# A two-layer transformer on one core: another fixed order for the second layer's steps

## The chip, the cores and the metric

The kernel runs on one core of a Trainium2 chip. A core has five engines with a queue of instructions each: TensorE (PE in the profile; its weight loads are shown apart as PEld), VectorE (DVE), ScalarE (ACT), GpSimd (POOL) and SyncE (SP, which here only starts DMAs). Each engine works off its own queue in order and waits at an instruction until what that instruction needs is there; while it waits, all that stands behind it in the queue waits too. The metric is the device time of one execution in microseconds (us): lower is better.

## The reference

The input x has 8 sequences of 256 rows of 512 values; a context of the same shape goes with it. Two layers follow each other, each with an attention and a feed-forward block that are added to x:

```python
x = x + tanh(g_xattn[0]) * causal_attention(layernorm(x), ctx, ctx)          # 16 heads of 32
x = x + tanh(g_ffn[0])   * ternary_ffn(layernorm(x), gate_up, proj)          # hidden 2048
x = x + tanh(g_xattn[1]) * cross_attention(layernorm(x), ctx, q_w, k_w, ...)  # 16 heads of 32
h = layernorm(x); h = h + out_8bit(silu(gate) * value)                       # hidden 2048
x = x + tanh(g_ffn[1]) * h
```

The change concerns the last three lines, "layer 1". There the queries are a linear layer of the normed x with an RMS norm behind it; each head's scores go through a softmax over 256 keys of the context; the result is projected and added. The feed-forward block quantizes its input and its hidden activation to 8 bits, each row by the row's own largest value: `scale = 127 / max|u|`, `round(u * scale)`. So a row's hidden values can only be quantized when all 2048 of them are there.

## The kernel before

Rows lie in 16 tiles `xs[0..15]` of 128 rows; a batch b (a sequence) is the two tiles 2b and 2b+1. Layer 1 is a software pipeline over batches. Pass b (of `for b in range(B)` at L1278) does the feed-forward block of batch b's two tiles (`first` = `feed1[2b]`, `second` = `feed1[2b+1]`) and, between its matmuls, parts of the attention of later batches.

*The order by hand.* `at(b, (n, step), ...)` puts a step at time b + n/16, and `timeline(*jobs)` (L1304) calls all steps sorted by these times. A pass has 16 units, and each unit begins with a gate product (`glu`, below); a step at 8.6 in `at(b, ...)` is emitted behind gate 8 of pass b, and one at 24.2 behind gate 8 of pass b+1. Steps from `at(b - 1, ...)` with n = 7.3 thus belong to the attention of batch b, emitted a pass ahead of its gates. PE executes its matmuls in exactly this order of emission. The queues of the other engines are put in order when the program is built, by the Tile framework's scheduler, which may move their instructions against each other as far as dependencies allow; on the chip each queue then is fixed.

*The steps of layer 1*, with the lines that the profile names:
- `glu(k)`, the gates: 8 matmuls (zT by gv weights) into one of two PSUM banks "gu"; ACT copies the bank to `gv` (L1186). After each odd one ACT takes a tanh (L1190), and DVE makes the gated value u from it (L1191, L1193) and its row maximum (L1194). 16 gates make a pass: 8 pairs, four for each of the two tiles. `gv` and `t1` have two buffers each, `u` two.
- `Feed1.done`: `quantize` takes the maximum over u (L1203 to L1206 on DVE: the scale), rescales u on ACT (L1232, two halves) and rounds it on POOL (L1233) into `uq`, of which there is one; two steps `turn` transpose uq by DMA into `uT` (L1238); two steps `project` multiply 8 chunks each into a bank ("o" for the first tile of a batch, "py" for the second), and behind the second half `store` adds the bank to x on DVE (L1223) and writes x out. `second.last` replaces these at the very end, with transposes on PE and four quarters.
- `Feed1.ready`: the norm ahead of the block (L1137 and L1143 on POOL, L1145 to L1151 on DVE, then L1153 and L1154 on POOL), and a DMA transpose of its result into `zT`.
- `Attention1.ready`: layer norm, turn on PE, load of keys and values, the query linear (`first(0)`, `first(1)`: matmuls "lin", L696 on DVE, the square on ACT L697), its norm (`scale`, L706), and the turn of the queries.
- `looks`: `scores(g)` for the four groups of heads (queries by keys, row maximum L415 on DVE), `parts` (the maxima in pieces, POOL L427 to L434, tile `mz`) and `shift` (turned on PE as "nt").
- `weighs`: four times `exps(g)` (scores turned round, exponential on ACT L481) and `weigh(g)` (32 matmuls into the one bank "o", copied by ACT L505; from g = 1 on POOL adds the sums, L508), in the order exps0, exps1, weigh0, exps2, weigh1, exps3, weigh2, weigh3.
- `Attention1.done`: `invert` (reciprocal on DVE, L1008), `divide` (spreads the inverses on PE into "inv" banks that take the places of "o" and "py", multiplied on DVE L1022), and two steps `add` (output projection, L1029).

PSUM has eight banks: two pairs "s" (scores, turns, exponentials), two "gu", one "o", one "py". A product into "o" or "py" has to wait until the last reader of that bank is done, be it `store`'s L1223, a copy L505, or L1022 and L1029.

Of the kernel before, what the change touches and what calls it, by code (L numbers as in the profile page):

```python
# [45 lines left out]
ALU = mybir.AluOpType  # L46
# [4 lines left out]
P = 128  # L51
B, S, D = 8, 256, 512
NT = B * S // P
NH, HD = 16, 32
DC = D // P
# [34 lines left out]
def flamingo_kernel(  # L90
# [24 lines left out]
    nc = tc.nc  # L115
# [10 lines left out]
    def bank(tag, shape=(P, 512), dtype=F32, name=None):  # L126
        pool, n = part_ps[tag]
        return pool.tile(list(shape), dtype, tag=tag, name=name or tag, bufs=n)
# [15 lines left out]
    def reach(i, n):  # L144
        assert stage.get(i, 0) == n - 1, (i, n)
        stage[i] = n
# [114 lines left out]
    pe = Tensor()  # L261
# [84 lines left out]
    def linear(dst, srcT, i, w):  # L346

        for c in range(DC):
            pe.matmul(
                dst,  # L350
                lhsT=srcT[:, c, i * P : (i + 1) * P],
                rhs=w(c),
                start=(c == 0),
                stop=(c == DC - 1),
            )


    class Attention:
# [3 lines left out]
        n = 0  # L362
# [150 lines left out]
                [*(lambda g=g: self.scores(g) for g in range(DC)), self.parts, self.shift],  # L513
            )

        def weighs(self):


            def exps(g):
                self.exps(g)  # L520
                ps[g] = self.p

            ps = {}
            steps = [lambda: exps(0)]
            for g in range(DC):
                if g + 1 < DC:
                    steps.append(lambda g=g: exps(g + 1))
                steps.append(lambda g=g: self.weigh(g, ps.pop(g)))
            return self.counted(self.nready + DC + 2, steps)

        def finish(self, steps):
# [2 lines left out]
    class Attention0(Attention):  # L534
# [21 lines left out]
        def done(self):  # L556
            def add():

                t = pair((P, 2, D), name="back")
                sums = bank("o", (P, 2, P), name="sums")  # L560
                for i in range(2):
                    rows = slice(i * P, (i + 1) * P)
                    for c in range(DC):
                        pe.transpose(
                            t[:, i, c * P : (c + 1) * P], self.oT[:, c, rows], ident
                        )
                    pe.transpose(sums[:, i, :], self.sums[:, rows], ident)
                inv = small.tile([P, 2, DC, 4], F32, tag="inv", name="inv", bufs=2)
                nc.vector.reciprocal(
                    inv, sums.rearrange("p i (r g e) -> p i g r e", r=4, g=DC)[:, :, :, :, 0]  # L570
                )
                for i in range(2):
                    xt = xs[2 * self.b + i]
                    w = self.oT[:, 2 * i : 2 * i + 2, :].rearrange("p c t -> p (c t)")
                    nc.vector.tensor_tensor(
                        w.rearrange("p (h c) -> p h c", h=NH),
                        t[:, i, :].rearrange("p (h c) -> p h c", h=NH),
                        inv[:, i].rearrange("p g r -> p (g r)").unsqueeze(2).broadcast_to([P, NH, HD]),
                        ALU.mult,
                    )  # L580
                    nc.vector.scalar_tensor_tensor(
                        xt, w, tg[:, 0:1], xt, ALU.mult, ALU.add
                    )
                    reach(2 * self.b + i, 1)

            return self.finish([add])
# [19 lines left out]
    def at(b, *steps):  # L606

        return [(b + n / 16, b + n / 16, [step]) for n, step in steps]
# [151 lines left out]
    with ExitStack() as part:  # L760
# [16 lines left out]
        a, z = att0[0], att0[1]  # L777
# [151 lines left out]
    def measure1(u):  # L929
        seen[0] += 1  # L930
        w = load1(u)
        a = q1.tile([P, QW], BF, tag="q", name="a1", bufs=2)
        behind(nc.scalar.activation(a, w, AF.Abs, accum_out=l1sum[:, u : u + 1]), block["A"])
# [17 lines left out]
    def quantize1(u):  # L951

        seen[1] += 1
        assert seen[0] == n1
        w = load1(u)
        _, dst, k = units1[u]
        ins = nc.gpsimd.tensor_scalar(w, w, wscale[:, k : k + 1], MAGIC, ALU.mult, ALU.add)  # L957
        behind(ins, block["P"])
        hold1()
        q = q1.tile([P, QW], BF, tag="q", name="q1", bufs=2)  # L960
        nc.gpsimd.tensor_scalar(q, w, 1.0, -MAGIC, ALU.mult, ALU.add)  # L961

        def hold():
            q8 = q1.tile([P, QW], F8, tag="q8", name="q8", bufs=2)
            nc.vector.tensor_scalar(q8, q, 1.0, -1.0, ALU.min, ALU.max, saturate=False)
            nc.sync.dma_start(out=dst, in_=q8.bitcast(U8))

        left.append(hold)
# [6 lines left out]
    class Attention1(Attention):  # L975
# [30 lines left out]
        def done(self):  # L1006
            def invert():
                nc.vector.reciprocal(self.oT[:, DC + 1, :], self.sums)  # L1008

            def divide():  # L1010
                for k in range(2):
                    w = bank(("o", "py")[k], (P, 2, S), name="inv")
                    for j in range(2):
                        pe.matmul(
                            w[:, j, :],
                            lhsT=spread[:, 2 * k + j, :],
                            rhs=self.oT[:, DC + 1, :],
                            start=True,
                            stop=True,
                        )  # L1020
                    cols = self.oT[:, 2 * k : 2 * k + 2, :]
                    nc.vector.tensor_tensor(cols, cols, w, ALU.mult)  # L1022

            def add(i):
                xt = xs[2 * self.b + i]
                nc.gpsimd.tensor_tensor(xt, xt, rob, ALU.add)
                t = bank(("o", "py")[i], name="proj")
                linear(t, self.oT, i, lambda c: wo[:, c, :])
                nc.vector.scalar_tensor_tensor(xt, t, tg[:, 1:2], xt, ALU.mult, ALU.add)  # L1029
                reach(2 * self.b + i, 3)  # L1030

            return self.finish([invert, divide, lambda: add(0), lambda: add(1)])

    att1 = [Attention1(b) for b in range(B)]
    x2 = ctx.enter_context(tc.tile_pool(name="x2", bufs=1, side="right", reuse_waits="tile"))
# [6 lines left out]
    with ExitStack() as part:  # L1042
# [4 lines left out]
        def rows(b):  # L1047
# [3 lines left out]
        jobs = [  # L1051
            (0.5, 3.0, [lambda u=u: measure1(u) for u in range(n1)]),
            (3.05, 3.05, [scales1]),
            (3.1, 6.5, [lambda u=u: quantize1(u) for u in range(n1)]),
            (6.6, 6.6, [hold1]),
        ]
# [44 lines left out]
    spread = w1p.tile([P, DC, P], F32, name="spread")  # L1101
# [176 lines left out]
    jobs = []  # L1278
    for b in range(B):
        first, second, a = feed1[2 * b], feed1[2 * b + 1], att1[b]  # L1280
        end = b == B - 1
        jobs += at(b, *((k, step) for k, step in enumerate(first.glus() + second.glus())))

        far = {B - 1: (15.9, 15.9), B - 2: (15.95, 15.95), B - 3: (13.2, 17.3)}.get(b, (13.2, 18.2))
        jobs += at(b, *zip((7.4 if b == B - 2 else 8.6, 9.6, 9.8, *far), first.done()))
        if end:
            jobs += at(b, (16.0, second.last))
        else:
            far = {B - 2: (23.9, 23.9), B - 3: (21.2, 22.2)}.get(b, (21.2, 24.2))
            jobs += at(b, *zip((17.4, 18.4, 18.6, *far), second.done()))  # L1290
        if b >= 2:

            late = 15.6 if b == 2 else 16.2
            jobs += at(b - 3, *zip((3.6, 12.2, 12.5, 14.2, late, 16.5, 18.9), a.ready()))
            jobs += at(b - 2, *zip((4.4, 6.4, 7.4, 9.3, 10.4, 14.1), a.looks()))
        if b >= 1:
            steps = (-0.8, 0.6, 2.3, 2.5, 3.2, 3.4, 4.2, 5.0) if end else (-0.8, 1.2, 3.2, 3.4, 4.2, 5.6, 6.2, 7.2)
            jobs += at(b - 1, *zip(steps, a.weighs()))
        steps = (5.1, 6.9, 7.6, 8.2) if end else (7.3, 9.2, 10.2, 11.2)
        jobs += at(b - 1, *zip(steps, a.done()))  # L1300
        for n, f in zip((7.7, 8.4) if end else (10.3, 13.0), (first, second)):
            norm, turn = f.ready()
            jobs += at(b - 1, (n, norm), (n + 1.7, turn))
    timeline(*jobs)  # L1304
# [52 lines left out]
```

## Time and profile before

| | us |
|---|---|
| median of 3 runs | 1248.93 (1246.83 to 1250.46) |
| the profiled execution, its device time | 1244.33 |
| its span in the profile | 1242.6 |
| layer 1 begins at about | 780 |
| second weighing done, passes in turn | 811.79, 869.8, 930.1, 990.24, 1050.7, 1110.98 |
| inverses of the last attention on PE | 1173.65 |
| first gate of the last pass | 1196.68 |

The six times of the second weighing mark the pipeline's passes: after the first they follow each other by 60.1 to 60.5 us. In the profile's timeline each line has a start, a duration, the engine, the line of the kernel, the operation and its operands; in brackets stands how long the engine had been idle before and which instruction released it. The view by windows gives for a stretch of time the busy time of each engine and the clock that TensorE was granted, as a share of full speed.

### The profile page before, as it was taken

How to read it: one execution, taken by the hardware profiler on the slowest of the kernel's cores; microseconds unless marked ns; L12 is line 12 of the kernel's file. 1: busy time of each engine (PE TensorE's matmuls, PEld its weight loads, DVE VectorE, ACT ScalarE, POOL GpSimd, SP SyncE). 2: the span in 40 equal slices, each digit the busy share in tenths (PEclk: the TensorE clock that was granted, in tenths of full speed). 3: DMA queues.
4: the chain of work that ended last, by engine and by line, in shares of the span. 5: the costliest groups of instructions: out<-in, count | busy, mean ns of one | idle time of the engine just before them, and what ended most of it. 6: DMA issues, size and time to landing. Idle time of an engine off the chain costs nothing.

```text
span 1242.6 us, 29878 instructions
## 1 busy us (share of the span) xinstructions
PE 1113.8 (90%) x12466; PEld 725.7 (58%) x12565; DVE 823.0 (66%) x1776; ACT 611.2 (49%) x1108; POOL 550.0 (44%) x821
## 2 busy tenths in 40 slices
PE   7988977799999897888999998899999999999976
PEld 3444433577777666666666775455555555555553
DVE  5677797764656455375654645777777777768684
ACT  3446547356575533433344453356464645464663
POOL 3333224353343556465564424826263535424250
PEclk9998888899999998999999999999999999999998
DMA  8343424622333233223222002311212121211231
GB/s 320 127 137 114 158 85 119 221 61 96 120 99 118 64 99 82 82 70 95 84 76 66 19 18 71 109 52 31 64 35 60 35 61 35 61 35 31 39 51 43
DMA packets 101767, 103.91 MB, mean 84 GB/s; under 512 B 61312, under 2 KB 72576, under 8 KB 101632
## 3 DMA queue, kind: packets, MB, share of 16 engines
q1 hardware_dynamic: 98608, 97.01, 26.6%
q10 hardware_dynamic: 3024, 4.98, 1.3%
q8 instruction: 98, 1.61, 0.5%
q14 instruction: 37, 0.30, 0.1%
HBM read 72.09 MB, written 15.73 MB: 71 GB/s over the span
## 4 chain that ended last, share of the span: by engine, by line
PE 29%; DVE 27%; POOL 12%; ACT 8%; issue 5%; DMA 1%; POOLq 0%; DVEq 0%; ACTq 0%
PE gu L256 10%; PE o L256 5%; PE s L256 5%; DVE nm L415 4%; PE y L256 3%; PE py L256 2%; DVE u L1193 2%; DVE h L843 2%; POOL acc L850 2%; DVE ln_st L277 2%; POOL w L957 2%; DVE t L1191 2%; DVE h L842 2%; POOL q L961 2%; DVE umax L1194 2%
## 5 line engine op out<-in xcount | busy, mean ns | idle before, releaser
L256 PE MATMUL gu<-xT,gu 128*128 128x128 f16 x4096 | 254.9, 221 | 11.7 <-DVE h L843 8.3
L256 PEld LDWEIGHTS <-gu 128*128 128x128 bf16 x4096 | 237.7, 99 | 42.2 <-issue 18.6
L850 POOL TENSOR_TENSOR acc<-acc,h 128x256 f32<-128x256 f32 x112 | 83.5, 745 | 130.6 <-ACT h L848 127.0
L256 PE MATMUL gu<-gv,zT 128*128 128x256 fp8e4 x1024 | 131.4, 274 | 10.9 <-ACT gv L1186 6.4
L1186 ACT COPY gv<-gu 128x512 f32<-128x512 f32 x128 | 74.0, 585 | 116.2 <-PE gu L256 108.3
L256 PEld LDWEIGHTS <-zT 128*128 128x128 bf16 x1024 | 96.0, 98 | 57.4 <-issue 36.7
L845 ACT CAST hs<-h 128x256 f16<-128x256 f32 x128 | 51.7, 404 | 147.0 <-DVE h L843 146.6
L842 DVE SCALAR_TENSOR_TENSOR h<-h,gu 128x256 f32<-128x256 f32 x128 | 53.3, 416 | 102.3 <-ACT h L841 97.0
L256 PE MATMUL y<-pr,hs 128*128 128x512 bf16 x413 | 113.5, 383 | 6.9 <-issue 1.4
L270 POOL TENSOR_TENSOR rs_r<-rs_t,mhalf 128x1 f32<-128x1 f32 (+1 forms) x88 | 60.7, 694 | 129.0 <-DVE rs_t L268 108.1
L481 ACT ACTIVATE p<-s 128x768 f32<-128x768 f32 (+1 forms) x128 | 109.8, 908 | 15.1 <-PE s L256 15.1
L415 DVE TENSOR_REDUCE nm<-s 128x4 f32<-128x1024 f32 x64 | 75.8, 1217 | 33.9 <-PE s L256 33.9
L848 ACT ACTIVATE h<-h,hid 128x256 f32<-128x256 f32 x112 | 56.6, 507 | 70.1 <-POOL hs L295 46.6
L508 POOL TENSOR_TENSOR oT<-oT 128x256 f32<-128x256 f32 x48 | 35.3, 735 | 124.3 <-ACT oT L505 124.1
L256 PE MATMUL s<-qT,kT 32*128 32x256 f32 (+1 forms) x1024 | 78.2, 377 | 2.5 <-DVE rs_t L268 1.1
L295 POOL TENSOR_TENSOR hs<-h,hs 128x256 f16<-128x256 f32 x64 | 44.5, 695 | 77.8 <-ACT hs L845 77.8
L841 ACT ACTIVATE h<-gu 128x256 f32<-128x256 f32 x128 | 48.5, 379 | 56.9 <-PE gu L256 56.7
L1191 DVE SCALAR_TENSOR_TENSOR t<-t,gv 128x512 f32<-128x512 f32 x64 | 46.4, 725 | 41.6 <-ACT t L1190 41.6
L256 PE MATMUL s<-kT,qT 32*128 32x256 f32 (+1 forms) x1024 | 68.9, 378 | 2.0 <-DVE nm L415 1.3
L407 DVE TENSOR_REDUCE nm<-s 128x2 f32<-128x256 f32 (+1 forms) x128 | 62.9, 551 | 11.6 <-PE s L256 11.3
L256 PE MATMUL o<-p,v 128*32 128x256 f32 (+1 forms) x1024 | 64.2, 370 | 5.8 <-DVE x L1223 5.6
L256 PEld LDWEIGHTS <-hs 128*128 128x128 f16 x512 | 45.6, 101 | 35.4 <-issue 4.7
(185 smaller groups left out, 2195.4 us busy)
## 6 DMA issues: line engine op xcount, KB each, us to landing
w<-in_gvT_dram SPq DMA_DIRECT2D x32, 512.0 KB, 3.8
w<-in_guT_dram SPq DMA_DIRECT2D x32, 256.0 KB, 3.0
w<-in_outT_dram SPq DMA_DIRECT2D x16, 512.0 KB, 3.6
cT<-in_cxT_dram SPq DMA_DIRECT2D x8, 512.0 KB, 4.9
x<-in_x_dram SPq DMA_DIRECT2D x16, 256.0 KB, 6.6
kT<-in_cxT_dram SPq DMA_DIRECT2D x8, 512.0 KB, 4.0
v<-in_cx_dram SPq DMA_DIRECT2D x8, 512.0 KB, 3.8
vd<-v SPq DMA_DIRECT2D x8, 512.0 KB, 5.3
```

The lines of the kernel that those rows point to most:

```text
L256: return self.kept(nc.tensor.matmul(*args, **kwargs))
L270: nc.gpsimd.tensor_tensor(r[:, :n], t[:, :n], mhalf[:, :n], ALU.pow)
L407: nc.vector.tensor_reduce(nm[:, :, qb], s[j][:, :, at[qb] : at[qb] + to[qb]], AX.X, ALU.max, negate=True,)
L415: nc.vector.tensor_reduce(nm, s[j].rearrange("p r (q k) -> p r q k", q=2), AX.X, ALU.max, negate=True)
L481: exp[0] = nc.scalar.activation(self.p[j], s[j][:, :, 0:n], AF.Exp)
L841: block["A"] = nc.scalar.activation(h, gu[:, 0], AF.Tanh, scale=0.5 / UP0)
L842: nc.vector.scalar_tensor_tensor(h, h, 1.0, gu[:, 0], ALU.add, ALU.mult)
L845: nc.scalar.copy(hs[:, 0], h)
L848: nc.scalar.activation(sq, h, AF.Square, scale=hid[:, 1:2])
L850: block["P"] = nc.gpsimd.tensor_tensor(self.acc[i], self.acc[i], sq, ALU.add)
L1186: nc.scalar.copy(self.gv[:, :, k % 2, :], gu)
L1191: nc.vector.scalar_tensor_tensor(t, t, 1.0, g, ALU.add, ALU.mult)
```

## The change

Only the order of emission in layer 1 changes; PE's, DVE's, ACT's and POOL's instructions are the same in number and kind. `weighs(late=True)`, in all passes but the last, swaps the last exponentials and the third weighing (exps3 behind weigh2). `divide` becomes two steps, one for each bank. The times n of nearly all attention steps are others: the weighings and exponentials are spread more evenly, the inverses and both projections lie a unit later, the query linear's second half and turn a unit later, the scores later. The second product half of `first` goes from 18.2 to 15.4, that of `second` from 24.2 to 23.2. At the end, the two products of the second tile of batch 6 move from 23.9 to 31.9, so that all 16 gates of the last pass stand ahead of both remaining products of 16 matmuls and `last`.

In the built program the first PE instruction that differs lies in the output projection of batch 0, where layer 1's pipeline starts; all before it is unchanged. In the changed file the lines lie up to two further down (L1232 is L1233 there, L1008 is L1010).

```diff
-        def weighs(self):
+        def weighs(self, late=False):
...
                 steps.append(lambda g=g: self.weigh(g, ps.pop(g)))
+            if late:
+                steps[5:7] = steps[6], steps[5]
...
-            def divide():
-                for k in range(2):
-                    w = bank(("o", "py")[k], (P, 2, S), name="inv")
-                    for j in range(2):
...
+            def divide(k):
+                w = bank(("o", "py")[k], (P, 2, S), name="inv")
+                for j in range(2):
...
-            return self.finish([invert, divide, lambda: add(0), lambda: add(1)])
+            return self.finish([invert, *(lambda f=f, k=k: f(k) for f in (divide, add) for k in range(2))])
...
-        far = {B - 1: (15.9, 15.9), B - 2: (15.95, 15.95), B - 3: (13.2, 17.3)}.get(b, (13.2, 18.2))
+        far = {B - 1: (15.95, 15.95), B - 2: (15.95, 15.95)}.get(b, (13.2, 15.4))
         jobs += at(b, *zip((7.4 if b == B - 2 else 8.6, 9.6, 9.8, *far), first.done()))
         if end:
             jobs += at(b, (16.0, second.last))
         else:
-            far = {B - 2: (23.9, 23.9), B - 3: (21.2, 22.2)}.get(b, (21.2, 24.2))
+            far = {B - 2: (31.9, 31.9), B - 3: (21.2, 22.2)}.get(b, (21.2, 23.2))
             jobs += at(b, *zip((17.4, 18.4, 18.6, *far), second.done()))
         if b >= 2:
-            late = 15.6 if b == 2 else 16.2
-            jobs += at(b - 3, *zip((3.6, 12.2, 12.5, 14.2, late, 16.5, 18.9), a.ready()))
-            jobs += at(b - 2, *zip((4.4, 6.4, 7.4, 9.3, 10.4, 14.1), a.looks()))
+            head = b == 2
+            turn, far = (11.25, 15.6) if head else (12.3, 17.2)
+            jobs += at(b - 3, *zip((3.6, turn, 12.5, 14.2, far, 17.5, 20.3), a.ready()))
+            jobs += at(b - 2, *zip((5.3, 7.3, 9.2, 11.3, 11.6, 14.1), a.looks()))
         if b >= 1:
-            steps = (-0.8, 0.6, 2.3, 2.5, 3.2, 3.4, 4.2, 5.0) if end else (-0.8, 1.2, 3.2, 3.4, 4.2, 5.6, 6.2, 7.2)
-            jobs += at(b - 1, *zip(steps, a.weighs()))
-        steps = (5.1, 6.9, 7.6, 8.2) if end else (7.3, 9.2, 10.2, 11.2)
+            steps = (-0.8, 0.6, 2.3, 2.5, 3.2, 3.4, 4.2, 5.0) if end else (-1.1, 0.2, 2.2, 3.2, 4.2, 6.2, 6.3, 8.2)
+            jobs += at(b - 1, *zip(steps, a.weighs(not end)))
+        steps = (5.1, 6.9, 6.9, 7.6, 8.2) if end else (8.3, 11.1, 11.15, 11.2, 12.2)
         jobs += at(b - 1, *zip(steps, a.done()))
-        for n, f in zip((7.7, 8.4) if end else (10.3, 13.0), (first, second)):
+        for n, f in zip((7.7, 8.4) if end else (11.35, 14.0), (first, second)):
```

More of the change, by code (lines that the diff above doesn't have):

```diff
@@ L1008, in invert @@
                 nc.vector.reciprocal(self.oT[:, DC + 1, :], self.sums)
-            def divide():
-                for k in range(2):
-                    w = bank(("o", "py")[k], (P, 2, S), name="inv")
-                    for j in range(2):
[L1014 to L1022, printed above, removed]
+            def divide(k):
+                w = bank(("o", "py")[k], (P, 2, S), name="inv")
+                for j in range(2):
+                    pe.matmul(
+                        w[:, j, :],
+                        lhsT=spread[:, 2 * k + j, :],
+                        rhs=self.oT[:, DC + 1, :],
+                        start=True,
+                        stop=True,
+                    )
+                cols = self.oT[:, 2 * k : 2 * k + 2, :]
+                nc.vector.tensor_tensor(cols, cols, w, ALU.mult)
             def add(i):
```

## The prediction

> **What bounds the kernel now.** I read the page first. TensorE (PE) is busy for 90% of the span, and the chain that ended last names it most often:
>
> ```profile
> PE 1113.8 (90%) x12466; PEld 725.7 (58%) x12565; DVE 823.0 (66%) x1776; ACT 611.2 (49%) x1108; POOL 550.0 (44%) x821
> ...
> PE 29%; DVE 27%; POOL 12%; ACT 8%; issue 5%; DMA 1%; POOLq 0%; DVEq 0%; ACTq 0%
> ```
>
> But the diff touches layer 1 alone, the part from some 780 us on, so I asked the trace for windows there: two stretches of the steady passes, the end, and two slices of 4 us in it (start:end, length, then PE, weight load, DVE, ACT and POOL busy, the granted clock, DMA share, GB/s).
>
> ```profile
> 920.00:980.00 60.00, 56.52 (x507) 34.02 (x505) 45.94 (x90) 31.72 (x47) 27.89 (x42) 1.00 0.19 49
> 1041.00:1101.00 60.00, 56.58 (x507) 34.11 (x506) 44.49 (x83) 31.29 (x47) 27.68 (x40) 1.00 0.19 49
> 1161.00:1243.00 82.00, 65.14 (x460) 39.38 (x452) 52.63 (x113) 40.29 (x60) 21.78 (x27) 0.92 0.20 44
> 1204.00:1208.00 4.00, 2.29 (x14) 1.41 (x12) 2.00 (x4) 3.40 (x5) 2.09 (x2) 0.76 0.26 49
> 1208.00:1212.00 4.00, 3.04 (x9) 1.01 (x8) 3.16 (x6) 1.31 (x2) 0.00 (x0) 0.50 0.44 82
> ```
>
> PE does 56.5 us of work in a pass of 60.4; DVE has 14 us to spare and ACT 28. So an order can win at most the 3.7 us that PE stands still, and can lose whatever the other queues make it wait. PE's timeline of one pass (start, us, what; in brackets the idle time before and its releaser) has the whole 3.73:
>
> ```profile
> 984.23 1.07 PE L256 MATMUL o<-p,v 128*32 128x256 f32 x16 [1.16 <-DVE x L1223]
> ...
> 1009.18 1.13 PE L256 MATMUL inv<-oT,spread 128*128 128x256 f32 x4 [1.51 <-DVE x L1223]
> ...
> 1031.56 1.05 PE L256 MATMUL gu<-gv,zT 128*128 128x256 fp8e4 x8 [0.45 <-DMA zT<-zq]
> ...
> 1033.22 3.70 PE L256 MATMUL lin<-wq,xT 128*128 128x512 f32 x8 [0.61 <-DVE lin L696]
> ```
>
> ACT's timeline shows how near the next stall is. The rescale of u (L1232) waits for DVE's scale, and all of ACT's later work stands behind it:
>
> ```profile
> 1002.27 0.59 ACT L505 COPY oT<-o 128x512 f32<-128x512 f32 x1 [0.61 <-PE o L256]
> 1004.25 0.59 ACT L1186 COPY gv<-gu 128x512 f32<-128x512 f32 x1 [1.38 <-DVE amax L1204]
> 1008.50 2.37 ACT L1232 ACTIVATE u<-u,magic,s 128x1024 f32<-128x1024 f32 x2 [3.67 <-DVE s L1206]
> 1010.78 0.56 ACT L1186 COPY gv<-gu 128x512 f32<-128x512 f32 x1
> ```
>
> Here the last weighing's copy (L505) is out before the wait; only gate copies stand behind it, and two "gu" banks cover them.
>
> **The change, part by part.** PE's instructions, their count and their durations stay; what moves is which of them waits for whom.
>
> *What it takes away.* `second`'s second product half is one gate earlier, so the weighing at 984.23 no longer waits for x (1.16). The inverses go into banks whose x is long done (1.51). The second norm's transpose and L696 come later against their users (0.45 and 0.61). All four may go: −3.73 a pass.
>
> *What it puts in their place.* The built program of the changed kernel gives each queue's order. ACT now has: gate 8's copy, **the rescale of `first`, then the last weighing's copy (L505)**, then gate 9's copy. DVE has the x of the odd tile (waits for the product half) ahead of gate 7's three steps, a row maximum, and only then the scale. I replayed one pass by hand, with t = 0 at the transposes of the queries. Durations are this trace's: gate 0.88 on PE, weighing 1.86, product half 1.73, copy 0.59, tanh 0.72, DVE's gate steps 0.69 to 0.74 each, row maximum (L415) 1.13 net of overlap, reciprocal 1.75, scale chain about 1, rescale pair 2.37, exponential pair 1.9, L508 0.75.
>
> 1. PE ends the product half at 11.6. DVE had been idle since 7.75, because x stands first in its queue: x 12.4, gate steps 14.5, L415 15.6, a second L415 16.9, scale 17.7. ACT rescales 17.75 to 20.1, copies the weighing by 20.65 and gate 9 by 21.2. Gate 11 needs gate 9's bank: PE waits 18.73 to 21.2, **2.47**. The two L415 cost PE 0.45 more at the exponentials and scores that wait for them.
> 2. POOL's uq pair ends 3.5 after the rescale began, at 21.25 (1008.50 to 1012.0 in this trace). The last sum (L508) stands behind it: 22.0. DVE's queue has t of gate 9 (22.65) before the reciprocal: 24.35. PE was ready at 22.1: **2.3**.
> 3. Ahead of the products with the inverses DVE has an L415 and two gate steps; the first output projection starts at 27.65 instead of 26.5: **1.15**.
> 4. POOL's mz now stands behind the steps of the norm (L1137, L1143, L1153, L1154): done 41.5, PE at 40.85: **0.7**.
> 5. The linear's norm comes late too: its sum L696 stands behind z of the second norm (POOL, 46.2), 48.0 to 48.7; ACT's square (L697) behind that, then exps0 49.4 to 51.3. PE waits **1.25**. `second`'s scale comes at 56.5, its rescale holds ACT until 58.85, and a gate's tanh, DVE's two steps and L697 again (63.0) hold the first weighing's copy to 64.1 and exps2 to 66.5: PE waits **0.65** at the "o" bank and **1.2** at the transposes of the next pass.
>
> Sum 10.2 instead of 3.73: a pass of 66.8 instead of 60.4. Steps 1 and 2 follow from the fixed queue order alone and I hold them nearly certain. Steps 4 and 5 pile up small delays, each with about 1 us of slack that a replay can misjudge: between nothing and 4 us a pass. I take my replay's 3.8, since before's own ACT wait of 3.67 shows that such a chain does arrive late.
>
> *Other edits.* `late` swaps the third weighing and the last exponentials: PE's and ACT's work stays, the swap alone is free while scores wait for neither. The split `divide` changes emission only. SP stores x ahead of loading v: v is used a pass later, nothing. The start of layer 1: the second weighing is done at 811.0 instead of 811.79, −0.8.
>
> *The end.* In the last pass all 16 gates now run before the two products of 16 matmuls. Gates alone run at DVE's 2.1 us a pair (L1191, L1193, L1194) instead of being spread with products; the rescale of x14 comes some 20 us after the first gate (at 1196.7), its two transposes land 5.7 and 9.3 later (as 1203.45 to 1209.17 and 1212.8 show), and the last tile's uq is at about 1228.8 instead of 1231.1: **−2.3**. Bounds: −5 if PE idles nowhere before `last`; +3 if the transposes then hold all of PE, with no gate left for cover.
>
> **The sum.** Five intervals from second weighing to second weighing took 299.2 (811.79 to 1110.98; the first is 58.0, as its window shows 2.2 us less PE work). Mine take 6.4 more each (10.2 − 3.73): +32. From there to the inverse of the last attention (1173.65, 62.7 later) the same steps come once more, all but the 1.2 at the next transposes: 6.4 − 1.2, +5. With −0.8 and −2.3: **+34**. The profiled execution took 1244.33, span 1242.6; it lies 4.6 below the median of 1248.93, so 1278 by it and **1283** by the median, which I take.
>
> [...] The granted clock is 1.00 through the steady passes, with gaps up to 1.5 us, but 0.76 and 0.50 in the two slices above, whose gaps are 1.14, 1.71 and 0.95. [...]
>
> DVE's u step (L1193) took 0.69 mostly, but 1.12 at 1026.55 while POOL was busy. [...] By the row, one more u step beside POOL in step 4 adds 1.12 − 0.69 = 0.43 a pass. My sum leaves both out; the range holds them.
>
> **The rivals.**
> - *Only steps 1 to 3 cost* (20%). 2.47 + 0.45 + 2.3 + 1.15 = 6.4 a pass against 3.73 is +2.6, over six passes +16, with −3.1 from the ends: 1262. For it: ACT is busy 32 us of 60 and can catch up. Against: the second rescale holds ACT once more.
> - *More than replayed* (12%): a slower clock after the gaps, or POOL and DVE in each other's way; 2 us more a pass, 1294, up to 1300 and beyond. For it: the slice with 0.50. Against: the clock of 1.00 throughout the steady passes.
> - *Other side: ACT isn't held* (10%). If `first`'s rescale starts by 13.1, it ends before the last weighing's copy is due; then steps 1 to 3 vanish and the four waits are gone: −0.8 − 6 × 3.73 − 2.3 = −25.5 gives 1223. It needs the scale 4.6 us earlier than I have it; from there each us later costs about one. For it: the edits do take away the four waits that the timeline shows. Against: x cannot come before the product half ends at 11.6.
> - *It doesn't do what it says* (5%): new waits equal old ones, 1249.
>
> **How the numbers follow.** Likeliest, 53%: steps 1 to 5 as replayed, own range 1272 to 1295. The whole range: low 1252 takes in the rival of steps 1 to 3 with a fifth of its waits hidden (1.3 a pass, 8 in all) and the end at its bound of −5; high 1300 takes in most of the third case. A measurement of this kernel can tell about 0.3% from no change. Faster 0.10 is the other side; same 0.05; slower 0.85.
>
> **What would show it.** In the changed profile: ACT's rescale of `first` with an idle time of 3 us or more, released by DVE's scale, right before an L505; a PE wait of about 2.5 at a gate, released by ACT's gate copy; a wait of about 2.3 at the inverse, released by DVE's reciprocal; the four old waits gone; passes of 66 to 67 us; POOL's mz behind L1154. I am wrong if the scale ends before the last weighing is done, if the two gaps coincide into one, or if passes stay near 60.

## The result

The changed kernel takes 1295.17 us (four runs, 1291.76 to 1300.34) where the kernel before takes 1247.88: a ratio of 1.038, 95% interval 1.034 to 1.043. That is 47 us slower; 1283 had been forecast, in a range of 1252 to 1300. The profiled execution is the slowest of the four: 1300.34 with a span of 1298.6, 56 us over the span shown of before. Of these 3.75 lie in layer 0, whose instructions did not change (the inverses of batch 0's attention start at 780.70 instead of 776.95), and are no work of the change; in runs 1 to 9 below, with the same layer 0, they start at 776.82 to 780.50. The two profiled executions lie apart by more than the medians do: before's is 3.6 us below its median, this one 5.2 above. So an account by these two profiles adds up to 56, not to 47.

The page's engine line and the chain of the changed kernel, which answer to the two shown of before:

```profile
PE 1153.8 (89%) x12466; PEld 746.9 (58%) x12565; DVE 821.7 (63%) x1776; ACT 609.8 (47%) x1108; POOL 544.2 (42%) x821
...
PE 34%; DVE 22%; POOL 13%; ACT 9%; issue 5%; DMA 1%; POOLq 0%; DVEq 0%; ACTq 0%
```

PE's instruction count is the same, but its busy time is 40 us longer (1153.8 against 1113.8). So by the page most of the loss is not PE standing still: groups of the same matmuls took longer. The view by windows shows a large part of why. First a stretch as before, then five passes, each from one transposition of the queries to the next (the columns are those of before; the clock is the third number from the end):

```profile
920.00:980.00 60.00, 53.77 (x465) 32.92 (x463) 37.89 (x76) 31.52 (x45) 24.60 (x38) 0.92 0.22 49
...
813.25:881.91 68.66, 60.70 (x494) 35.63 (x490) 44.69 (x88) 31.50 (x46) 23.65 (x39) 0.93 0.16 39
881.91:953.48 71.57, 65.16 (x510) 38.63 (x507) 47.40 (x91) 32.24 (x47) 28.55 (x43) 0.90 0.19 41
953.48:1025.02 71.54, 65.31 (x510) 38.49 (x507) 46.09 (x89) 32.10 (x46) 27.22 (x42) 0.90 0.20 41
1025.02:1093.48 68.46, 62.07 (x510) 37.13 (x507) 45.08 (x89) 31.44 (x46) 25.83 (x41) 0.95 0.22 43
1093.48:1162.87 69.39, 63.49 (x511) 37.75 (x507) 45.26 (x85) 31.64 (x47) 24.19 (x39) 0.93 0.22 43
```

Passes of 68.5 to 71.6 us instead of 60.4, and a granted clock of 0.90 to 0.95 where it had been 1.00. PE's timeline of the pass from 953.48 has the waits:

```profile
974.67 1.03 PE L256 MATMUL gu<-gv,zT 128*128 128x256 fp8e4 x8 [1.93 <-ACT gv L1187]
977.82 3.78 PE L256 MATMUL inv<-oT,spread 128*128 128x256 f32 x8 [2.11 <-DVE oT L1010]
981.39 4.89 PE L256 MATMUL proj<-wo,oT 128*128 128x512 f32 x8
...
1007.54 1.71 PE L256 MATMUL s<-qT,kT 32*128 32x256 f32 x6 [2.08 <-ACT p L481]
```

The four waits of before (for x, x, zT and lin) are gone. Three others have come: at gate 11, at the inverses, at the second exponentials (1.93, 2.11 and 2.08 here; 1.93 to 2.77, 1.28 to 2.11 and 1.43 to 2.08 in the five passes). Behind them the matmuls are slow: the pair of inverses takes 3.78 where two halves took 1.03 and 1.13 before, the projection 4.89 instead of 3.60. Windows of 2 us behind the first two waits and the third show the clock at half:

```profile
977.00:979.00 2.00, 1.18 (x3) 1.01 (x4) 2.00 (x3) 0.09 (x1) 0.00 (x0) 0.54 0.31 57
979.00:981.00 2.00, 2.00 (x7) 1.55 (x6) 2.00 (x4) 0.00 (x0) 0.00 (x0) 0.50 0.00 0
981.00:983.00 2.00, 2.00 (x4) 0.98 (x3) 1.56 (x4) 0.00 (x0) 0.00 (x0) 0.50 0.00 0
983.00:985.00 2.00, 2.00 (x5) 0.91 (x4) 0.65 (x1) 0.00 (x0) 0.00 (x0) 0.75 0.00 0
...
1009.00:1011.00 2.00, 2.00 (x19) 1.01 (x12) 1.31 (x3) 1.29 (x3) 0.00 (x0) 0.50 0.00 0
```

Why PE waits at gate 11 is in ACT's and DVE's timelines. ACT stands at the rescale of `first` for 3.20 until DVE's scale is there; behind it come the last weighing's copy and gate 9's copy, which holds the bank that gate 11 needs:

```profile
971.30 2.37 ACT L1233 ACTIVATE u<-u,magic,s 128x1024 f32<-128x1024 f32 x2 [3.20 <-DVE s L1207]
973.57 0.56 ACT L505 COPY oT<-o 128x512 f32<-128x512 f32 x1
974.04 0.58 ACT L1187 COPY gv<-gu 128x512 f32<-128x512 f32 x1
```

DVE's scale is late because x stands first in its queue and waits for PE's product half; gate 7's three steps, two row maxima and the scale follow without a gap:

```profile
965.45 0.75 DVE L1224 SCALAR_TENSOR_TENSOR x<-py,g,x 128x512 f32<-128x512 f32 x1 [4.15 <-PE py L256]
...
971.11 0.15 DVE L1207 TENSOR_TENSOR s<-s,back 128x1 f32<-128x1 f32 x1
```

At the end, the last pass's first gate starts at 1257.69, so 40.9 us before the end of the span; before it was 45.9 (1196.68 to 1242.6). The two products now follow all gates, with one wait for the transposes between them:

```profile
1277.21 3.62 PE L256 MATMUL py<-ou,uT 128*128 128x512 fp8e4 x16
1283.22 5.31 PE L256 MATMUL py<-ou,uT 128*128 128x512 fp8e4 x16 [2.40 <-DMA uT<-uq]
```

Of the 56 us: layer 0 +3.75; the start of layer 1 −2.3 (second weighing done at 813.25, less 3.75, against 811.79); five passes +50.4 (349.6 against 299.2); from there to the last attention's inverses +9.1 (71.8 against 62.7); to the last pass's first gate 0.0 (23.03 both times); the end −5.0.

### The profile page after: what moved, and what is told of

Same layout as the page of the kernel before. It is cut to its first block, busy times and chain, and to the rows that moved or that the text cites. A ratio compares the mean times of both kernels' runs of the same rounds, so it can differ in the third digit from the quotient of the medians.

```text
span 1298.6 us, 29871 instructions
## 1 busy us (share of the span) xinstructions
PE 1153.8 (89%) x12466; PEld 746.9 (58%) x12565; DVE 821.7 (63%) x1776; ACT 609.8 (47%) x1108; POOL 544.2 (42%) x821
## 4 chain that ended last, share of the span: by engine, by line
PE 34%; DVE 22%; POOL 13%; ACT 9%; issue 5%; DMA 1%; POOLq 0%; DVEq 0%; ACTq 0%
PE gu L256 11%; PE s L256 5%; PE o L256 5%; PE y L256 3%; DVE nm L415 2%; PE proj L256 2%; PE py L256 2%; PE inv L256 2%; DVE ln_st L277 2%; POOL acc L852 2%; DVE h L845 2%; POOL rs_r L270 2%; POOL w L959 2%; DVE h L844 2%; PE lin L256 2%
## 5 line engine op out<-in xcount | busy, mean ns | idle before, releaser
L256 PE MATMUL gu<-gv,zT 128*128 128x256 fp8e4 x1024 | 137.1, 282 | 18.7 <-ACT gv L1187 17.4
L256 PE MATMUL s<-qT,kT 32*128 32x256 f32 (+1 forms) x1024 | 89.6, 388 | 13.7 <-ACT p L481 10.4
L1234 POOL TENSOR_SCALAR uq<-u 128x1024 bf16<-128x1024 f32 x30 | 31.3, 1045 | 131.2 <-ACT u L1233 130.1
L256 PEld LDWEIGHTS s<-qT,kT 32*128 32x128 f32 x1024 | 49.8, 193 | 38.9 <-ACT p L481 14.0
```

The source lines that it names most:

```text
L256: return self.kept(nc.tensor.matmul(*args, **kwargs))
```

## Experiments

Times are medians, ratios to the kernel before on the same chip, with 95% intervals. "Pass" is the distance from one transposition of the queries to the next.

**1. The end alone, in the kernel before.**

```diff
-        far = {B - 1: (15.9, 15.9), B - 2: (15.95, 15.95), ...
+        far = {B - 1: (15.95, 15.95), B - 2: (15.95, 15.95), ...
-            far = {B - 2: (23.9, 23.9), ...
+            far = {B - 2: (31.9, 31.9), ...
```

> The kernel before with the end of the change alone (the last two products of the second tile of batch 6 at 31.9, those of the last first tile at 15.95). Theory: the end is worth what the changed kernel's last pass shows, 40.9 us from first gate to end of span instead of 45.9, so -5.0: 1243 where before is 1248. Rival: the gain belonged to the other order of the queues there and is gone on its own: 1248 within 0.3%.

Measured: 1242.99 against 1247.68, 0.996 (0.994 to 0.998). The end is a gain of its own, of 4.7 us.

**2. Is it the clock? Fillers on PE in the changed kernel.** Small matmuls on constants stand where PE waits.

```diff
+    def fill(n):
+        w = bank("py", (P, 2, S), name="fill")
+        for _ in range(n):
+            pe.matmul(w[:, 0, :], lhsT=ident_b, rhs=warm, start=True, stop=True)
...
+            jobs += at(b - 1, (0.15, lambda: fill(16)), *((n, lambda: fill(16)) for n in (() if end else (10.9, 11.05))))
```

> The changed kernel with 16 small matmuls on constants, into the free bank py, at each of the three places of a pass where PE waits (ahead of gate 11, of the inverses, of the second exponentials). PE's waits on other engines stay; only PE does not stand still in them. Theory that the lowered clock is the larger loss (PE busy 62 to 65 us a pass for 56.6 us of work): busy time without the fillers returns to 57, the clock to 1.00 in the steady passes, 5 to 8 us a pass, 1255 to 1265. Theory that the waits themselves are the loss and the clock only follows: 1290 or more. A filler that is too long costs up to 1 us a pass.

Measured: 1305.51, 1.047 (1.043 to 1.050): slower than the changed kernel, though the clock is 0.98 to 1.00. But it isn't a clean test. With the fillers in, DVE's queue came out in another order: more of gate 9's and gate 11's steps (the maximum of gate 9, u of gate 11) stand ahead of the first product with the inverses (L1023), and the projection got a new wait, behind which it took 5.35 where the same pass's other projection took 3.60:

```profile
979.96 1.99 PE L256 MATMUL inv<-oT,spread 128*128 128x256 f32 x8 [0.36 <-DVE oT L1010]
984.27 5.35 PE L256 MATMUL proj<-wo,oT 128*128 128x512 f32 x8 [2.32 <-DVE oT L1023]
```

The inverses take 1.99 instead of 3.78, which the fillers were to show. The time says nothing of the clock alone; runs 5 and 6 repeat it as a pair with DVE's order fixed, in all passes but the first.

**3. ACT's order alone.** The rescale of `first` stands behind the tanh of gate 9, and the step that emits it goes from 8.6 to 9.05, behind that tanh; the step has no PE instruction.

```diff
-                    behind(nc.scalar.activation(u, u, AF.Identity, bias=magic, scale=sc), exp[0])
+                    r = behind(nc.scalar.activation(u, u, AF.Identity, bias=magic, scale=sc), exp[0])
+                    if self.i % 2 == 0:
+                        behind(r, tanh[0])
...
-        jobs += at(b, *zip((7.4 if b == B - 2 else 8.6, 9.6, 9.8, *far), first.done()))
+        jobs += at(b, *zip((7.4 if b == B - 2 else 9.05, 9.6, 9.8, *far), first.done()))
```

> The changed kernel with ACT's rescale of first ordered behind the tanh of gate 9 (and so behind the last weighing's copy and the copy of gate 9). Theory that this rescale's place is the knot: the waits of 1.93 at gate 11 and 2.11 at the inverse and the lowered clock behind them go, some 4 + 3.5 us a pass; the wait of 2.08 at the second exponentials stays: 1250 to 1258. Rival: the inverse stays late because DVE is behind with row maxima and gates, or uq comes too late for the product at 13.2: 1275 or more.

Measured: 1285.21, 1.029 (1.025 to 1.033): 10 us better than the changed kernel, where 37 to 45 had been expected; the rival holds. The waits at gate 11 and at the inverses are gone, but the next one in the chain has taken their place, again with slow matmuls behind it (5.40 for this projection, 3.60 for the pass's other one; the pass's clock is 0.95):

```profile
968.55 1.89 PE L256 MATMUL inv<-oT,spread 128*128 128x256 f32 x8
973.71 5.40 PE L256 MATMUL proj<-wo,oT 128*128 128x512 f32 x8 [3.26 <-DVE oT L1024]
```

DVE's timeline has a gate step, a row maximum, a gate step, a row maximum and a third gate step between the reciprocal (966.50) and the product with the inverses (972.98).

**4. ACT's and DVE's order.** DVE's steps of gates 9 and 11 are emitted behind both products with the inverses and kept there.

```diff
+                if self.i % 2 and k in (1, 3) and 1 < self.i < NT - 1:
+                    self.gated.append(gated)
+                else:
+                    gated()
...
+            jobs += at(b, (11.18, lambda f=second: [g(divided[0]) for g in f.gated]))
```

> The changed kernel with ACT's rescale of first behind the tanh of gate 9, as in the run before, and DVE's steps of gates 9 and 11 behind both products with the inverses (L1023). Theory that the wait of 3.26 at the output projection in that run is DVE's order and nothing else: it falls below 1, the clock stays 1.00 there; the wait of 2.08 at the second exponentials and the half clock behind it stay: passes of 61 to 63 us, 1248 to 1258. Rival, that DVE is simply late with all its work: the wait moves on to the next scores or gates, passes stay at 65 or more, 1275 or more.

Measured: 1252.49, 1.004 (1.002 to 1.007), and from the second pass on passes of 60.8 to 62.2: the time is as expected. One part is not: the wait at the second exponentials, which was to stay at 2.08, is 1.08 to 1.16 in three of these passes and 0.58 in the last, and their clock is 1.00 in all but the first of them (0.97). A pass and this wait in it:

```profile
1005.20:1066.19 60.99, 58.84 (x510) 34.88 (x506) 45.60 (x91) 31.81 (x47) 28.24 (x42) 1.00 0.21 49
...
1051.72 0.70 PE L256 MATMUL s<-qT,kT 32*128 32x256 f32 x4 [1.08 <-ACT p L482]
```

The first pass, which DVE's edit leaves out, took 69.3, with 3.35 at the projection and 2.08 at the second exponentials. ACT's order alone gave 10 us, DVE's alone (run 5) 14, both together 43: each alone leaves or uncovers the other's wait.

**5 and 6. DVE's order alone, without and with fillers.** Run 5 has run 4's edit of DVE's order without ACT's; run 6 adds the fillers of run 2.

> The changed kernel with DVE's order mended alone (gates 9 and 11 behind L1023), ACT's as it was. The waits at gate 11 (1.93) and at the inverses (about 1.4, as the reciprocal no longer stands behind a gate step) stay, with half clock behind them: 1280 to 1292. It is the pair to the next run.

> As the run before, with fillers on PE at the three waits (15 and 15 small matmuls at gate 11 and the inverses, 14 at the second exponentials). Theory that the half clock is a loss of its own, set by PE standing still: the waits on ACT and DVE end when they did, but the work behind them runs at full clock: 4 to 7 us a pass less than its pair, 1250 to 1268. Rival, that what PE would gain by the clock it loses to the same queues a little later, as in the first run with fillers: within 5 us of its pair.

Measured: 1280.76, 1.026 (1.024 to 1.029), as expected, with waits of 1.93 and mostly 1.63 from the second pass on; and with fillers 1284.47, 1.030 (1.027 to 1.032). Here are three passes of the first and two of the second:

```profile
881.37:948.48 67.11, 60.76 (x506) 36.13 (x507) 45.74 (x90) 31.44 (x47) 27.71 (x42) 0.97 0.17 44
948.48:1013.91 65.43, 59.26 (x510) 34.86 (x507) 45.70 (x90) 31.41 (x47) 27.68 (x42) 1.00 0.18 45
1013.91:1081.21 67.30, 61.96 (x511) 36.65 (x507) 46.70 (x91) 32.59 (x48) 29.42 (x43) 0.95 0.18 44
```

```profile
885.16:951.12 65.96, 63.97 (x551) 39.19 (x551) 45.61 (x90) 31.41 (x47) 27.68 (x42) 1.00 0.23 45
951.12:1017.28 66.16, 63.96 (x551) 39.18 (x551) 45.79 (x90) 31.42 (x47) 27.68 (x42) 1.00 0.17 45
```

Two things follow. With the fillers PE's longest waits in the second to fourth pass are 0.55 instead of 1.93, and the clock is 1.00 there, as in the fifth; in the first pass, where DVE's order is not mended and the fillers bring back run 2's wait of 2.32 at the projection, it is 0.98. And yet next to nothing is won: the time is within 5 us of its pair, as the rival said. The 3.7 us more are no price of the clock: by the profiles the first pass is 2.3 longer and begins 1.5 later, while the four passes behind it took 264.9 us against 266.1, so 0.3 less each where 4 to 7 had been expected. The pass of run 5 that happened to keep its clock (65.43) is only 1.7 to 1.9 us shorter than its neighbours, and the fillers cost 0.5 to 1 themselves. Where PE waits for the same queues a little later, part of what a half clock costs is time that it would have waited anyway: in the pass at 0.95 PE is busy for 2.7 us more than in the one at 1.00, and the pass is 1.9 longer.

**7. The square's order.** On top of run 4, ACT's square of the query linear's first half (L699) goes behind the first exponentials; it had stood ahead of them and waited for DVE's L698.

```diff
+            if later and i == 0:
+                later.append(square)
+            else:
+                square()
...
+            jobs += at(b - 3, (15.5 if head else 16.05, lambda a=a: a.later.pop()()))
```

> As the run with both orders mended, and ACT's square of the query linear's first half (L699) behind the first exponentials instead of ahead of them. Theory that the wait of 2.08 at the second exponentials is this square, which waits for z on GpSimd and DVE: it goes, and with it the last drop of the clock in the steady passes: passes of 57 to 58 us, 1220 to 1230, below the kernel before. Rival: the exponentials wait for something else (nt, L445) or the late square delays the next norm: 1245 or more.

Measured: 1241.67, 0.996 (0.995 to 0.998). The wait at the second exponentials is gone, and from the second pass on passes are 59.0 to 59.5 at clock 1.00. The expected 1220 to 1230 was not reached: that wait had been 0.58 to 1.16 and not 2.08 in run 4's steady passes, these are now only 1 us shorter than before's, and the first pass took 63.7. There DVE's mended order had been left out, and the old wait of 3.35 at the projection, with a clock of 0.69 and 0.74 in the two windows of 3 us from 835 on, was still there.

**8. All passes mended.** The same with the first pass of layer 1 included.

```diff
-                if self.i % 2 and k in (1, 3) and 1 < self.i < NT - 1:
+                if self.i % 2 and k in (1, 3) and 0 < self.i < NT - 1:
```

> The run with ACT's, DVE's and the square's order mended, with DVE's order mended in the first pass of layer 1 too, where it was left out and the output projection waited 3.35 us with half clock behind it. Theory: the first interval falls from 63.7 by the 5 to 6 us that the wait and the clock cost: 1235 to 1237. Rival: the wait returns elsewhere in that pass: 1241 as before.

Measured: 1236.34, 0.991 (0.988 to 0.994): as expected, and the fastest of all. Its first pass and a steady one:

```profile
812.68:870.88 58.20, 55.48 (x495) 33.06 (x491) 42.58 (x87) 30.80 (x45) 22.99 (x38) 1.00 0.19 46
...
990.21:1049.18 58.97, 58.09 (x511) 34.59 (x507) 45.72 (x91) 32.07 (x47) 28.78 (x43) 1.00 0.22 50
```

So the change's order in time is sound; with three pins on other engines' queues it beats the kernel before by 11 us, some 5 of them from the end.

**9. The row maxima.** On top of run 8, DVE's steps of gate 7 stand behind the maxima of the scores at 7.3.

> As that, and DVE's steps of gate 7 behind the row maxima of the scores at 7.3, so that the last exponentials and the scores at 9.2 find their banks free. Theory that the 0.45 and 0.43 that are left there, and the part that the profile counts as busy matmuls, are these maxima: 1 to 1.6 us a pass, 1227 to 1232. Rival, that the scale of first then comes later and ACT's copies behind its rescale with it: no gain or a loss, 1236 or more.

Measured: 1239.89, 0.994 (0.991 to 0.997); from the second pass on passes of 59.2 to 60.2. No gain, as the rival had it, but the wait that took its place is another: the 0.45 and 0.43 that run 8 has in two of its passes are gone, and the projection now waits 0.8 to 1.13 for DVE's product with the inverses in each pass, where it had waited 0.65 in every other one from the second on. So the maxima did hold PE up, and moving them only moved the wait.

**10 to 12. How long may PE stand still?** The kernel before gets one hole on PE a pass, where nothing else waits.

```diff
+    def hole():
+        w = bank("py", (P, 2, S), name="fill")
+        pe.matmul(w[:, 0, :], lhsT=ident_b, rhs=warm[:, 0:S], start=True, stop=True)
+        for _ in range(2):
+            nc.gpsimd.tensor_scalar(warm, warm, 1.0, 0.0, ALU.mult, ALU.add)
+        pe.matmul(w[:, 0, :], lhsT=ident_b, rhs=warm[:, 0:S], start=True, stop=True)
```

> The kernel before with one hole of about 2 us on PE in each of six passes, at 4.9 of a pass, where nothing else waits (PE waits for two GpSimd operations on a constant). Theory that a lone gap of 2 us lowers the clock as in the changed kernel: 2 us and 3 to 4 us of half clock behind it, 5.5 a pass, 1275 to 1285. [...]

> The kernel before with the hole on PE at 4.9 of a pass made by one GpSimd operation instead of two, some 1.3 us instead of 2.37. By the waits of 1.16 and 1.51 that the kernel before has at clock 1.00, the clock stays 1.00 and the hole costs at most its length: 7 in all, 1248 to 1255. If any hole there lowers the clock, as the one of 2.37 did: 1258 or more.

> The same hole from two GpSimd operations on 768 values instead of 1024, some 1.8 to 2.0 us, the size of the changed kernel's waits at gate 11. If the clock drops at this length too: more than its length a pass, 1258 to 1264. If it stays 1.00: 1.9 a pass at most, 1250 to 1258. It says whether the changed kernel's 1.93 could have lowered the clock alone, or only together with the 2.11 behind it.

Measured: 1266.63 for the long hole (1.017, 1.013 to 1.021), 1257.64 for the short one (1.009, 1.006 to 1.012), 1263.57 for the one between (1.013, 1.009 to 1.018). PE's timeline gives their lengths, 2.37, 1.23 and 1.94; one line and a pass's window of each, in that order:

```profile
934.39 0.27 PE L256 MATMUL fill<-warm,ident_b 128*128 128x256 bf16 x1 [2.37 <-POOL warm L1115]
...
921.59:986.25 64.66, 58.79 (x510) 34.90 (x509) 46.17 (x90) 31.95 (x47) 30.23 (x44) 0.97 0.19 46
```

```profile
1002.51 0.27 PE L256 MATMUL fill<-warm,ident_b 128*128 128x256 bf16 x1 [1.23 <-POOL warm L1115]
...
990.85:1053.24 62.39, 57.15 (x509) 34.40 (x508) 46.04 (x90) 31.91 (x47) 29.11 (x43) 1.00 0.19 48
```

```profile
1004.37 0.27 PE L256 MATMUL fill<-warm,ident_b 128*128 128x256 bf16 x1 [1.94 <-POOL warm L1115]
...
865.23:927.77 62.54, 57.11 (x509) 34.30 (x508) 46.19 (x90) 31.94 (x47) 29.79 (x44) 1.00 0.19 47
991.99:1056.17 64.18, 58.73 (x509) 34.70 (x508) 46.17 (x90) 31.94 (x47) 29.78 (x44) 0.97 0.18 46
```

The hole of 1.23 leaves the clock at 1.00 in all four steady passes looked at, that of 2.37 lowers it in all four (to 0.97), that of 1.94 in two of four (0.97; 1.00 in the others). Where it falls, PE's busy time is 1.6 us longer (58.8 against 57.1). So a lone hole of these two sizes can lower the clock, as the theory for the long one had it, but the drop behind it costs 1.6, not 3 to 4, and the run stays below the 1275 expected. The short hole came out between its two expectations: its clock stays up, yet its pass is 2.0 longer than before's 60.4, more than its length. From the hole's first matmul (1001.00) to the gate behind its second (1002.62) it takes 1.62 of PE's time, as its two matmuls add 0.4 to the wait. The rest is a longer wait further on, in three of the four passes: 0.92 and 0.88 for zT, where before has 0.38 and 0.45, and 1.47 for L696 instead of 0.88.

## Why the prediction was right, and where it was not

**The knot (steps 1 and 2): right, nearly to the tenth.** From the start of the pass at 953.48, DVE's scale came at 17.8 (replayed: 17.7), gate 9's copy ended at 21.1 (21.2), the uq pair at 21.3 (21.25), the reciprocal at 24.3 (24.35). The waits were 1.93 and 2.11 instead of 2.47 and 2.3. PE arrived 0.5 later at gate 11 than I had it, part of it spent at the scores at 970.24, which took 1.52 instead of 1.15; gate 11 started at 21.2 all the same, as ACT's copy sets it. So the 0.45 that step 1 added for the maxima was in its 2.47 already, and the sum had it twice. That the order of the queues is the cause, runs 3, 4, 7 and 8 show: with PE's order of emission unchanged, the loss of 47 us falls to 6 and then turns into a gain of 11, of which the end gives some 5.

**Step 3 (1.15 at the projection): there, but covered.** In the changed kernel the inverses ran at half clock (0.54 and 0.50 in the windows from 977 to 981) and took longer than DVE needed. With the wait before it gone (run 3) it came out, as 3.26: DVE's queue there was worse than replayed.

**Steps 4 and 5: sizes wrong, mostly.** mz was done just when PE came (0.0 instead of 0.7) in the pass from 953.48; PE waited 0.68 for it in the stretch to the last inverses, and 0.28 to 0.51 in three passes of run 5. The second exponentials waited 2.08 instead of 1.25, by the chain named: z, L698, the square, the exponentials. The two waits at the end of the pass (0.65 and 1.2) did not come. A PE slowed by its clock need not be the reason: at clock 1.00, in run 5's pass of 65.43 and in run 6's from the second on (there with DVE's order mended), PE waits there for 0.33 at most. Which step of the replay made them too large, the runs do not say.

**The clock: the term that was missing.** That the durations of PE's instructions stay did not hold: the pair of inverses took 3.78 instead of 2.16, and passes were 68.5 to 71.6, not 66 to 67. The sum had 0 for the clock; the rival "more than replayed" had 2 us a pass, a term that no run shows. By the profile the lower clock took more. At clock 1.00, a pass in this order has 59.3 us of busy PE (run 5's pass of 65.43); the five passes here have 60.7, 65.2, 65.3, 62.1 and 63.5, together some 23 us more than 59.3 each (57.0 in the first, which has 2.3 less work), or 4.6 a pass. Counted from transposition to transposition, five passes took 349.6 against 298.1 before, and these 51.5 divide into 23 of lower clock, 16 of more idle time (32.9 against 16.7) and some 13 that lie inside groups of matmuls which the page counts as busy (59.3 at full clock, against 56.7 before). These 13 are short waits, as far as run 5's pass shows: its 64 matmuls s<-qT,kT (the scores turned round) take 401 ns each, as before, and yet their groups fill 6.4 us instead of 5.0. The whole is an estimate, since run 5 has another order on DVE, and it is a division of the profile's time, and not what each would give back alone: runs 5 and 6 show that the clock by itself returned next to nothing (0.3 us a pass). The causal chain starts at the queues. So the total came out near for partly wrong terms, and that part is luck: the waits of steps 3 to 5 that did not come (3.7 a pass less 0.8) were made up for by the clock and by the short waits. The measured 1295.17 lies at the upper edge of the likeliest case (1272 to 1295). The rival "more than replayed" (1294), with its slower clock after the gaps, came closer in number and had the term that the sum lacked.

**The clock and the u step.** The prediction's rows of before had a clock of 0.76 and 0.50 beside gaps of 1.14, 1.71 and 0.95, so a lower clock was to be reckoned with, and it came: behind a lone gap of 2.37 it dropped each time, behind one of 1.94 in two passes of four, behind one of 1.23 not. The 0.43 for one more u step beside POOL played no part that these runs could tell: the u step (L1194) took 0.745 on the mean of the pass at 953, less than L1193 before (0.880 in the stretch from 920 to 980).

**The ends.** The start was −2.3 instead of −0.8. The end was −5.0 instead of −2.3, my bound and not my value: the first transpose of the last uq came 32.0 after the first gate instead of 34.9, which is 2.9 where 2.3 were forecast, and the last products ran at full clock (1.04 for four of them at 1290.72; 1.00 in the windows from 1289 to 1295) where before's had run at half (1.89 at 1232.70; 0.50 from 1232 to 1236), which gave 2.1 more. The stretch to the last inverses was +9.1 instead of +5: it has the waits of 1.93 and 2.11 again, 0.68 for mz and 1.39 for nT in place of the 2.08, and a clock of 0.93 instead of 1.00.

**The other side (10%)** needed the scale by 13.1; it came at 17.8, since x could not come before the product half.

What wasn't tried: the single edits within the steady passes (the swap of the last exponentials, the new places of the product halves) one at a time, and how the scheduler came to order ACT's and DVE's queues as it did.

## What to carry to other kernels

When an order is written out for one engine, read what the built program makes of the other engines' queues, and look there for an instruction that waits for something late with short, urgent ones behind it. Mend such knots together: one alone uncovers the next (10 and 14 us singly, 43 together). Where a new wait on PE is as long as those that lowered the clock here (1.94 in two passes of four, 2.37 in all four; 1.23 in none), price the clock behind it too (1.6 us here), but only as a bound: where PE waits for the same queues again a little later, little of it comes back (run 6).

## What the runs showed of the hardware

- How long the clock stayed at half can be estimated from windows of 2 us, taking it to be either 1.00 or 0.50, the lowest that any window shows. Behind the hole of 2.37 (run 10, from 933 on) they have 0.95, 0.50 and 0.70, which is 0.2 + 2.0 + 1.2 = 3.4 us at half; behind that of 1.94 (run 12, from 939 on) 0.93, 0.50 and 0.72, again 3.4. In the changed kernel's pass from 953.48 the four windows shown from 977 on give 1.84 + 2 + 2 + 1 = 6.8, twice that, and the four from 1007 on, behind the third wait, 6.8 again (0.72, 0.50, 0.50, 0.57); in the next pass it is 3.4 behind the first two waits (0.96, 0.50, 0.69) and 3.4 behind the third (0.64, 0.51). By this 3.4 us at half cost 1.7 us of PE's work, an estimate; behind the holes 1.6 was measured.
- The same wait does not always lower the clock: a hole of 1.94 did in two passes of four, and the waits of 1.93 and 1.63 with one gate between them left one pass of run 5 at 1.00 and two others at 0.97 and 0.95. What the waits have to meet for it, these runs do not say.
